# A Mamba layer's normalising and output products by column halves of TensorE, with the planner's TensorE prices by tiling and 62 moved kinds of operations

## The chip, the cores and the metric

The kernel runs on one core of a Trainium2 chip. The metric is the device time of one launch in microseconds. The kernel before takes 8540.97 us, the median of 3 runs (8536.66 to 8543.05). Of a core's engines the text names TensorE (PE; its weight loads are shown apart as PEld), VectorE (DVE), ScalarE (ACT), GpSimd (POOL) and SyncE (SP), whose queue issues most DMAs.

## The reference

The input x is 4 x 128 x 64 x 64 (four images of 128 channels, 4096 tokens each). Two layers follow each other; the first is what the change touches.

```python
# layer 0
x = x + conv_attn_hybrid(group_norm(x), ...)     # seed Mamba, cascade of two Mambas, convolution ffn
# layer 1
t = to_tokens(x)
t = t + attention(ln(t), ...)                    # 4 heads of 32
t = t + moe(ln(t), ...)                          # 8 experts, top 2
```

Layer 0 projects the image onto 8 seed channels and runs a small Mamba over them; it splits the normalised 128 channels into 8 groups of 16 and runs a cascade of two Mambas over each group; it mixes the groups and ends with an ffn that has a 3 x 3 depthwise convolution. One Mamba is:

```python
def _mamba(x, in_w, in_b, conv_w, conv_b, A_log, D, dt_bias, rms_w, out_w, headdim, d_state):
    zxbcdt = x @ in_w.T + in_b
    z, xBC, dt = ...                              # dt through softplus
    xBC = _silu(conv1d(xBC) + conv_b)             # causal, 3 taps
    xs, Bm, Cm = ...
    y = _ssd(xs * dt[..., None], dt * A, Bm, Cm)  # chunks of 64: Yd within, Yo from the carried state
    y = y + D[None, None, :, None] * xs
    y = y.reshape(b, l, di) * _silu(z)
    y = y * jax.lax.rsqrt(jnp.mean(y * y, -1, keepdims=True) + 1e-05) * rms_w
    return y @ out_w.T
```

The mean of y * y and the last product, y @ out_w.T, are the two products that the change reshapes.

## The kernel before

Tokens are worked on in blocks of 512 (LB), each of 8 chunks of 64 (Q). A block of one Mamba is an item. There are 8 seed items (all four images at once) and 64 cascade items: 4 images x 2 Mambas x 8 blocks, where the second Mamba of an image follows the first two blocks behind. The 8 channel groups of a cascade item are 8 lanes, in ng = 2 groups of four; a seed item has 4 lanes and ng = 1.

An item passes four stages, each a Python generator: outer (load x, normalise, split into a high and a low half, store to hl), prep (dt and its running sum acs), front (the input projections ps_z, ps_x, ps_B, ps_C; the masked product gm of B and C; the chunk states ps_st; their scan cd; the part ps_yo from the carried state) and back (the exponentials e from ps_d, their weighing with gm, the product of e and x in the PSUM banks that the profile calls bank and the code py, the gate zs, and at the end `product("ps_ms", ...)` and `product("ps_out", ...)`). At any step the back of one item, the front of the next, the prep of the one after and the outer of the one after that are recorded in turn, and beside them the ffn of the image before (stage ffn).

Nothing is issued while it is recorded. The class Deck collects every call as an Op; neighbouring TensorE calls with one output and one source become one Op (record, L800). `price` gives an Op a duration, from a formula or, for three tiles, from the table SIDE (L763) per matmul, and every TensorE Op has 0.1 us on top. `flush` (L879) then simulates the five engines: each takes, of its Ops whose inputs are there and whose buffers are free, the one first in line, and the order in which the Ops start is the order in which they are issued. The place in line is the recorded number plus an offset from BEHIND (L869), by stage and engine, or by stage, engine and tile: positive is later, negative earlier. One step of the scan records about 150 of them (the trace has some 4100 VectorE, 3000 ScalarE and 500 GpSimd instructions and 2400 groups of matmuls for 66 steps). [...] All recorded operations carry line L996 in the profile, the line that issues them, and are told apart by their tiles.

The two products (lines 699 to 704) add up over the lane groups in one PSUM tile: for each group a full 128 x 128 stationary operand whose columns outside that group's lanes are zero.

Buffers: gm has 3 (4 KB a partition each), xg (the loaded x) 3, acc (the convolution's sum) 2 plus depth, outs 3 plus depth; wide PSUM tiles (tag d: ps_z, ps_x, ps_B, ps_C, ps_ea, pt_b, ps_g, ps_st, ps_yo, ps_d) share 2. The ffn of the last image runs after the scan with depth 1, beside the projections of the attention, and is planned by a second flush.

Of the kernel before, what the change touches and what calls it, by code (L numbers as in the profile page):

```python
# [31 lines left out]
LB = 512  # L32
NBLK = L // LB
Q = 64
# [241 lines left out]
class Mamba:  # L276
# [161 lines left out]
    def front(self, it):  # L438
# [68 lines left out]
        for U in range(NU // 2):  # L507
# [29 lines left out]
            for i in range(2):  # L537
                for jj in range(2):
                    for g in range(ng):
                        for c in range(2):  # L540
                            t = 2 * (2 * U + i) + c
                            for q in range(2):
# [3 lines left out]
                                                 start=True, stop=True)  # L546
            gm = work.tile([128, 4, 2, ng * Q], F32, tag="gm", bufs=3, name="gm")
            nc.vector.tensor_mul(gm.rearrange("s a q x -> s q a x"), d.rearrange("s q u h g l -> s q (u h) (g l)"),
# [72 lines left out]
    def back(self, it, out):  # L621
# [77 lines left out]
        def product(name, lhsT, rhs):  # L699
            p = sh.ps(name)  # L700
            for g in range(ng):
                nc.tensor.matmul(p.rearrange("p (c u l) -> p c u l", c=2, l=Q), lhsT=lhsT[:, g, :], rhs=rhs[:, g],
                                 start=g == 0, stop=g == ng - 1)
            return p
# [45 lines left out]
class Op:  # L750
    __slots__ = ("engine", "calls", "cost", "deps", "users", "waits", "ready", "rank", "uses", "set",
                 "phase", "stage", "out", "src", "both")

    def __init__(self, engine):
        self.engine, self.calls, self.cost, self.deps, self.users = engine, [], 0.0, set(), []
        self.ready, self.rank, self.uses, self.set, self.phase = 0.0, 0.0, {}, None, None
        self.out = self.src = None
        self.both = False
# [3 lines left out]

SIDE = {"py": 0.030, "ps_yo": 0.0185, "ps_d": 0.08}  # L763


class Deck:
# [33 lines left out]
    def record(self, engine, name, args, kw):  # L800
# [8 lines left out]
        if not (op is not None and op.engine == engine and (  # L809
                engine == "tensor" and op.out == made and op.src == src or gelu and op.set == GELU)):  # L810
            op = Op(engine)
            op.out, op.src = made, src
            op.cost = 0.1 if engine == "tensor" else 0.0
            op.stage = self.stage
            op.phase = self.phase if engine in ("tensor", "scalar") else None
            self.ops.append(op)
# [17 lines left out]
    def price(self, engine, name, args, kw, out, ins, op):  # L834
# [4 lines left out]
        if engine == "tensor":  # L839
            tile = op.out.rsplit("_", 1)[0]  # L840
            if tile in SIDE:
                return SIDE[tile]
            lhs = kw.get("lhsT", ins[0])
            single = lhs.dtype == F32R
            side = (128 // max(32, lhs.ap[0][1])) * (128 // max(32, free(lhs)))
            if name == "transpose":
                return 0.12
            return max(0.0165, 0.00046 * n / side) * (1 if single else 2) * (1 if single or side > 1 else 1.85)
# [20 lines left out]
    BEHIND = {  # L869
        ("prep", "tensor"): 150, ("prep", "scalar"): 20,  # L870
        ("front", "vector"): 20,
        ("back", "vector"): -20,
        ("outer", "scalar"): 190, ("outer", "tensor"): -20, ("outer", "vector"): 60, ("outer", "gpsimd"): 60, ("outer", "sync"): 60,
        ("ffn", "vector"): 120, ("ffn", "scalar"): -10, ("ffn", "tensor"): -30, ("ffn", "gpsimd"): -30, ("ffn", "sync"): -30,
    }
    LAG = 0.2
    LAND = 4.0

    def flush(self, tc):  # L879
# [29 lines left out]
        for i, op in enumerate(ops):  # L909
            if op.waits == 0:  # L910
                heappush(events, (0.0, 0, i))
        now, table, lock = 0.0, None, None
        lockers = {"vector": 0.0, "gpsimd": 0.0}
        while events:
# [16 lines left out]
            for e in engines:  # L931
# [3 lines left out]
                while ready[e]:  # L935
# [12 lines left out]
                    if any(room[r] < k for r, k in need.items()) or any(  # L948
# [5 lines left out]
                        aside.append(key)  # L954
                        continue
                    chosen = key
                    break
# [10 lines left out]
                for t in [t for t in op.uses if t not in opening]:  # L968
                    opening.add(t)
                    room[self.ring_of[t]] -= 1  # L970
                    head[self.ring_of[t]] = head.get(self.ring_of[t], 0) + 1
                start = now
                if e == "scalar":
                    if op.set == SILU:
                        phases[op.phase] -= 1
                        lock = op.phase if phases[op.phase] else None
                    if op.set is not None and op.set != table:
                        table = op.set
                        start += 1.3
# [130 lines left out]
def layer0(tc, T, td, const, ident, eps, where, batches, qkv):  # L1110
# [9 lines left out]
    with ExitStack() as ctx:  # L1120
# [63 lines left out]
        def load(b, k, work=work):  # L1184
            xin = work.tile([128, LB], F32, tag="xg", bufs=3, name="xin")
            nc.sync.dma_start(out=xin, in_=T["x"][b, :, blk(k)])
            return xin
# [25 lines left out]
        class Seed:  # L1213
# [3 lines left out]
            def outer(self):  # L1217
# [4 lines left out]
                for b in range(NBATCH):  # L1222
                    normed(b, xs[b])
                    nc.tensor.matmul(pg[32 * b:32 * b + 32, :], lhsT=P("tok"), rhs=xs[b], start=True, stop=True)
                    if b < 2:
                        xs.append(load(b + 2, k))
                g = work.tile([128, LB], F32, tag="xg", bufs=3, name="g")
                nc.vector.tensor_scalar(g, pg, P("tokb"), None, ALU.add)
# [84 lines left out]
        def ffn(b, work, ps, depth=0, diag=0, taps=None, ps_taps=None):  # L1313
# [84 lines left out]
            def conv(k):  # L1398

                accs[k] = []  # L1400
                for g in range(2):
                    acc = work.tile([128, LB], F32, tag="acc", bufs=2 + depth, name="acc")
                    sums = made[k].pop(0) if k in made else None
# [90 lines left out]
        def single(tag, bufs):  # L1494
            return lambda name: pp.tile([128, LB], F32, tag=tag, bufs=bufs, name=name)

        pending = deck.staged("ffn", ffn(pending, last, single("f", 4), 1, 4, taps, single("t", 2)))
        run((pending, FFN), (deck.staged("early", early()), 5 * NBLK + 7))
# [503 lines left out]
```

## Time and profile before

| | us |
|---|---|
| median of 3 runs | 8540.97 |
| profiled execution, with what lies around its span | 8550.11 |
| its span | 8548.1 |
| TensorE busy over the span | 7815.6 (91%) |
| VectorE | 6321.3 (74%) |
| ScalarE | 5117.9 (60%) |
| GpSimd | 4775.4 (56%) |
| scan of the items with no ffn beside it, 348 to 1297: TensorE busy | 815.01 of 949.00 |
| scan with ffn beside it, 1297 to 3440: TensorE busy | 1877.58 of 2143.00 |
| last ffn and first projections, 3440 to 3880: TensorE busy | 380.23 of 440.00 |
| rest, attention and experts, 3880 to 8548: TensorE busy | 4516.45 of 4668.00 |

Shares over the whole span mix two stages: until about 3880 us the first layer, after it the attention, where GpSimd is over 90% busy. What is changed must be read from the first 3880 us. Durations of matmul records overlap, so a step is read from its start to the start of the next. The seed items come every 34 us, the cascade items every 47 to 57 us. The column after a bar is the engine's idle time before such instructions and what ended it.

### The profile page before, as it was taken

What the parts mean: (1) busy time and instruction counts of PE and PEld (TensorE: products, weight loads), DVE (VectorE), ACT (ScalarE), POOL (GpSimd) and SP (SyncE); (2) the same over time, 40 slices, a digit from 0 to 9 for tenths busy, and PEclk for the clock granted to TensorE, in tenths of its full rate; (3) what the DMA queues carried; (4) which work ended last, traced back from release to release, by engine and by line L of the source; (5) the groups of instructions that cost most, each with busy time, mean ns of one, the idle gap of its engine ahead of it and who ended that gap; (6) DMA issues with size and microseconds to landing.
All of it is one profiled execution on the core that took longest, in us unless ns stands there. A gap on an engine that the chain in (4) does not pass through costs nothing.

```text
span 8548.1 us, 191291 instructions
## 1 busy us (share of the span) xinstructions
PE 7815.6 (91%) x80284; PEld 4646.5 (54%) x80284; DVE 6321.3 (74%) x11211; ACT 5117.9 (60%) x6448; POOL 4775.4 (56%) x3225
## 2 busy tenths in 40 slices
PE   5888888888888888888999999999999999999998
PEld 3566666666666666644455555555555555555554
DVE  5666666787777777777777777777777777777775
ACT  5766666777677767764555555555555555555554
POOL 1111110111111111105999999999999999999997
PEclk8989999999989998998999999999999999999999
DMA  4211111111111111125554454545445445444442
GB/s 136 86 48 46 41 40 45 55 51 54 49 52 51 54 49 51 49 90 140 128 128 126 120 126 129 129 126 132 125 124 132 127 124 130 121 114 117 118 122 62
DMA packets 306604, 800.54 MB, mean 94 GB/s; under 512 B 43984, under 2 KB 61008, under 8 KB 288848
## 3 DMA queue, kind: packets, MB, share of 16 engines
q1 hardware_dynamic: 304848, 780.94, 34.7%
q8 instruction: 633, 10.37, 0.5%
q10 hardware_dynamic: 432, 5.12, 0.2%
q14 instruction: 227, 1.86, 0.1%
q0 software_dynamic: 464, 2.25, 0.1%
HBM read 595.19 MB, written 192.94 MB: 92 GB/s over the span
## 4 chain that ended last, share of the span: by engine, by line
PE 30%; POOL 20%; issue 3%; DVE 3%; ACT 1%; DMA 0%; POOLq 0%; DVEq 0%; SPq 0%; ACTq 0%
POOL s L1850 12%; PE ps_mx L1806 7%; PE acc L1865 6%; PE ps_s L1844 6%; POOL es L1852 5%; PE ps_s L1838 3%; PE ps_e L1754 2%; PE ps_den L1878 2%; DVE mx L1808 1%; PE ps_taps L996 1%; POOL parts L1668 0%; PE ps_sh L1825 0%; PE ps_f L1743 0%; POOL cx L1670 0%; PE ps_f L1742 0%
## 5 line engine op out<-in xcount | busy, mean ns | idle before, releaser
L1808 DVE TENSOR_REDUCE mx<-ps_mx 128x1 f32<-128x512 f32 x4096 | 2790.8, 689 | 815.1 <-PE ps_mx L1806 788.7
L1848 ACT ACTIVATE e<-ps_s 128x1024 f32<-128x1024 f32 x2048 | 1986.6, 1022 | 1722.1 <-PE ps_s L1844 1594.0
L1850 POOL TENSOR_TENSOR s<-e 128x1024 f32<-128x1024 f32 x1024 | 2442.6, 2385 | 217.8 <-ACT e L1848 214.0
L1806 PE MATMUL ps_mx<-k,q 128*128 128x512 f32 x4096 | 1881.1, 469 | 60.4 <-DVE mx L1808 28.0
L1852 POOL TENSOR_TENSOR es<-s 128x512 f32<-128x512 f32 x1024 | 1311.7, 1281 | 80.3
L1844 PE MATMUL ps_s<-q,k 128*128 128x512 f32 x4096 | 1282.4, 394 | 0.0
L1865 PE MATMUL acc<-e,V 128*32 128x512 f32 x8192 | 1095.2, 607 | 0.0
L1806 PEld LDWEIGHTS ps_mx<-k,q 128*128 128x128 f32 x4096 | 775.5, 189 | 531.8 <-DVE mx L1808 222.1
L1844 PEld LDWEIGHTS ps_s<-q,k 128*128 128x128 f32 x4096 | 773.5, 189 | 139.2 <-issue 2.9
L996 DVE SCALAR_TENSOR_TENSOR y<-bank,const,y 128x128 f32<-128x128 f32 (+1 forms) x1152 | 355.3, 338 | 589.0 <-PE bank L996 586.4
L996 DVE SCALAR_TENSOR_TENSOR e<-e,gm 128x1024 f32<-128x1024 f32 (+1 forms) x576 | 656.7, 1161 | 69.3 <-ACT e L996 68.5
L1838 PEld LDWEIGHTS ps_s<-mr,ones 32*128 32x128 f32 x4096 | 200.9, 181 | 890.8 <-ACT e L1848 418.7
L996 PE MATMUL bank<-e,xp 64*32 64x128 f32 x17408 | 592.9, 276 | 36.1 <-DVE y L996 27.0
L996 POOL TENSOR_TENSOR zs<-y,zs 128x1024 f32<-128x1024 f32 (+1 forms) x72 | 182.4, 2533 | 780.1 <-DVE y L996 780.0
L996 ACT ACTIVATE e<-ps_d 128x1024 f32<-128x1024 f32 (+1 forms) x576 | 548.1, 976 | 116.1 <-PE ps_d L996 107.1
L1838 PE MATMUL ps_s<-mr,ones 32*128 32x512 f32 x4096 | 532.1, 496 | 20.4 <-ACT e L1848 20.4
L996 PEld LDWEIGHTS bank<-e,xp 64*32 64x32 f32 x17408 | 439.2, 108 | 165.7 <-DVE y L996 58.4
L996 PE MATMUL ps_d<-rt,lt 32*128 32x256 f32 x4352 | 373.0, 307 | 26.8 <-ACT e L996 9.8
L996 POOL CAST x<-halo_casc 128x8 fp32r<-128x8 f32 x64 | 17.0, 266 | 663.8 <-PE ps_C L996 663.7
L996 POOL TENSOR_TENSOR u<-acs 128x512 f32<-128x512 f32 x72 | 75.8, 1053 | 516.0 <-DVE acs L996 465.3
L996 PEld LDWEIGHTS ps_d<-rt,lt 32*128 32x128 f32 x4352 | 271.1, 186 | 168.6 <-issue 56.7
L1865 PEld LDWEIGHTS acc<-e,V 128*32 128x32 f32 x8192 | 161.4, 108 | 364.2 <-issue 358.4
(349 smaller groups left out, 12260.5 us busy)
## 6 DMA issues: line engine op xcount, KB each, us to landing
k<-kd SPq DMA_DIRECT2D x512, 512.0 KB, 5.7
x<-hl SPq DMA_DIRECT2D x256, 256.0 KB, 4.0
V<-vd SPq DMA_DIRECT2D x128, 512.0 KB, 9.7
cd<-raw SPq DMA_DIRECT2D x256, 256.0 KB, 3.3
parts<-cd SPq DMA_DIRECT2D x128, 512.0 KB, 6.2
xin<-in_x SPq DMA_DIRECT2D x128, 256.0 KB, 3.2
q<-qd SPq DMA_DIRECT2D x512, 64.0 KB, 4.9
hl<-hi SPq DMA_DIRECT2D x72, 256.0 KB, 2.5
```

The costliest lines, as they stand in the source:

```text
L996: getattr(getattr(self.nc, op.engine), name)(*[self.real(a) for a in args], **{k: self.real(a) for k, a in kw.items()})
L1754: nc.tensor.matmul(pe, lhsT=xl[:, tok], rhs=ew[:, e:e + 2, :].rearrange("p e c -> p (e c)"), start=True, stop=True)
L1806: nc.tensor.matmul(p, lhsT=q4s[u][:, 128 * qt:128 * qt + 128], rhs=k4s[u][:, blk(kb)], start=True, stop=True)
L1808: nc.vector.tensor_reduce(mxs[u][:, qt, kb:kb + 1], p, AX.X, ALU.max)
L1838: nc.tensor.matmul(pts[j // 2][:, j % 2, :], lhsT=ones2[rows, :], rhs=mrows[u][rows, :], start=True, stop=False)
L1844: nc.tensor.matmul(pts[j // 2][:, j % 2, :], lhsT=k4s[u][:, 128 * kt:128 * kt + 128], rhs=q4s[u], start=False, stop=True)
L1848: nc.scalar.activation(e[:, 2 * j:2 * j + 2], pts[j], AF.Exp)
L1850: nc.gpsimd.tensor_add(s2, e[:, 0:2], e[:, 2:4])
L1852: nc.gpsimd.tensor_add(s, s2[:, 0], s2[:, 1])
L1865: nc.tensor.matmul(accs[u][32 * j:32 * j + 32, :], lhsT=Vs[u][:, 4 * g + j, :], rhs=e[:, j, :], start=g == 0, stop=g == 7)
L1878: nc.tensor.matmul(p[32 * j:32 * j + 32, :], lhsT=ones, rhs=s, start=True, stop=True)
```

## The change

`product` writes each lane group's rows of the output (64 of 128 partitions with ng = 2) by its own matmul with a stationary operand of 128 x 64, each with start and stop, and no longer adds up. In the planner, the calls that write the two py banks are joined even where their source e changes; SIDE's values for py and ps_yo are raised; each TensorE Op has a mode (rows and columns of its stationary operand), and 0.1 us is added where it differs from the one before; a candidate in the same mode could be taken first within NEAR places, which is 0. BEHIND has 62 new entries in place of its 14. gm has 2 buffers, xg 4, acc one more; the last ffn runs with depth 0.

```diff
--- before.py
+++ after.py
@@ -544,7 +544,7 @@
                                 nc.tensor.matmul(d[64 * c:64 * c + 64, q, i, jj, g, :],
                                                  lhsT=Bt[rows, 2 * g + jj, t, :], rhs=Ct[rows, 2 * g + jj, t, :],
                                                  start=True, stop=True)
-            gm = work.tile([128, 4, 2, ng * Q], F32, tag="gm", bufs=3, name="gm")
+            gm = work.tile([128, 4, 2, ng * Q], F32, tag="gm", bufs=2, name="gm")
             nc.vector.tensor_mul(gm.rearrange("s a q x -> s q a x"), d.rearrange("s q u h g l -> s q (u h) (g l)"),
                                  const("tri")[:, None, None, 0:ng * Q].to_broadcast([128, 2, 4, ng * Q]))
             gms.append(gm)
@@ -697,10 +697,12 @@
             return t.rearrange("p (u g c l) -> p g c u l", u=NU, g=ng, c=2)
 
         def product(name, lhsT, rhs):
-            p = sh.ps(name)
+
+            p, n = sh.ps(name), 128 // ng
             for g in range(ng):
-                nc.tensor.matmul(p.rearrange("p (c u l) -> p c u l", c=2, l=Q), lhsT=lhsT[:, g, :], rhs=rhs[:, g],
-                                 start=g == 0, stop=g == ng - 1)
+                rows = slice(n * g, n * g + n)
+                nc.tensor.matmul(p[rows].rearrange("p (c u l) -> p c u l", c=2, l=Q), lhsT=lhsT[:, g, rows],
+                                 rhs=rhs[:, g], start=True, stop=True)
             return p
 
         pm = product("ps_ms", self.ms, by_token(y))
@@ -749,18 +751,18 @@
 
 class Op:
     __slots__ = ("engine", "calls", "cost", "deps", "users", "waits", "ready", "rank", "uses", "set",
-                 "phase", "stage", "out", "src", "both")
+                 "phase", "stage", "mode", "out", "src", "both")
 
     def __init__(self, engine):
         self.engine, self.calls, self.cost, self.deps, self.users = engine, [], 0.0, set(), []
         self.ready, self.rank, self.uses, self.set, self.phase = 0.0, 0.0, {}, None, None
-        self.out = self.src = None
+        self.out = self.src = self.mode = None
         self.both = False
 
 
 SILU, GELU, EXPS = "silu", "gelu", "exps"
 
-SIDE = {"py": 0.030, "ps_yo": 0.0185, "ps_d": 0.08}
+SIDE = {"py": 0.0435, "ps_yo": 0.033, "ps_d": 0.08}
 
 
 class Deck:
@@ -807,7 +809,7 @@
         op = self.ops[-1] if self.ops else None
         gelu = AF.Gelu_apprx_tanh in args
         if not (op is not None and op.engine == engine and (
-                engine == "tensor" and op.out == made and op.src == src or gelu and op.set == GELU)):
+                engine == "tensor" and op.out == made and (op.src == src or made != out.tensor.name) or gelu and op.set == GELU)):
             op = Op(engine)
             op.out, op.src = made, src
             op.cost = 0.1 if engine == "tensor" else 0.0
@@ -838,9 +840,10 @@
             return 0.06
         if engine == "tensor":
             tile = op.out.rsplit("_", 1)[0]
+            lhs = kw.get("lhsT", ins[0])
+            op.mode = max(32, lhs.ap[0][1]), max(32, free(lhs))
             if tile in SIDE:
                 return SIDE[tile]
-            lhs = kw.get("lhsT", ins[0])
             single = lhs.dtype == F32R
             side = (128 // max(32, lhs.ap[0][1])) * (128 // max(32, free(lhs)))
             if name == "transpose":
@@ -867,13 +870,31 @@
 
 
     BEHIND = {
-        ("prep", "tensor"): 150, ("prep", "scalar"): 20,
-        ("front", "vector"): 20,
-        ("back", "vector"): -20,
-        ("outer", "scalar"): 190, ("outer", "tensor"): -20, ("outer", "vector"): 60, ("outer", "gpsimd"): 60, ("outer", "sync"): 60,
-        ("ffn", "vector"): 120, ("ffn", "scalar"): -10, ("ffn", "tensor"): -30, ("ffn", "gpsimd"): -30, ("ffn", "sync"): -30,
+        ("back", "gpsimd", "last0_casc1"): 120, ("back", "scalar"): -50, ("back", "scalar", "A_casc1"): -200,
+        ("back", "scalar", "e"): -40, ("back", "sync", "gfd"): -10, ("back", "sync", "hl"): 120,
+        ("back", "sync", "raw"): -40, ("back", "sync", "td"): 110, ("back", "tensor", "ps_d"): -70,
+        ("back", "tensor", "py"): 120, ("back", "vector", "A_casc1"): -200, ("back", "vector", "bdt_casc1"): 70,
+        ("back", "vector", "biasB_casc1"): 40, ("back", "vector", "wc_casc1"): -120, ("ffn", "scalar"): 10,
+        ("ffn", "tensor", "ps_mean"): 40, ("ffn", "vector", "acc"): 140, ("front", "gpsimd"): 220,
+        ("front", "gpsimd", "last_casc1"): -10, ("front", "scalar"): 20, ("front", "scalar", "Bc"): 50,
+        ("front", "scalar", "Cc"): -200, ("front", "scalar", "cd"): 200, ("front", "scalar", "zs"): -70,
+        ("front", "tensor"): 20, ("front", "tensor", "ps_ea"): -120, ("front", "tensor", "ps_g"): -120,
+        ("front", "tensor", "ps_st"): -20, ("front", "tensor", "pt_x"): 40, ("front", "vector", "gm"): 10,
+        ("front", "vector", "ps_st"): -20, ("front", "vector", "xd"): -200, ("front", "vector", "xp0"): -10,
+        ("outer", "gpsimd"): -200, ("outer", "gpsimd", "halo_seed"): 200, ("outer", "gpsimd", "last0_casc0"): 120,
+        ("outer", "scalar"): 40, ("outer", "scalar", "hi"): -120, ("outer", "scalar", "ln_r"): -20,
+        ("outer", "sync", "raw"): 20, ("outer", "sync", "wc_seed"): 20, ("outer", "sync", "xin"): -40,
+        ("outer", "tensor"): 110, ("outer", "tensor", "ps_tok"): 40, ("outer", "vector"): -20,
+        ("outer", "vector", "A_seed"): 200, ("outer", "vector", "W_casc0"): 200, ("outer", "vector", "bdt_casc0"): 10,
+        ("outer", "vector", "bdt_seed"): 10, ("outer", "vector", "biasB_casc0"): 20,
+        ("outer", "vector", "biasB_seed"): -10, ("outer", "vector", "biasx_seed"): 200,
+        ("outer", "vector", "raw"): 70, ("prep", "gpsimd"): 70, ("prep", "gpsimd", "cdx"): 10,
+        ("prep", "gpsimd", "halo_seed"): 10, ("prep", "gpsimd", "x4"): -40, ("prep", "scalar", "cde"): -70,
+        ("prep", "sync", "x4"): 40, ("prep", "tensor", "ps_cd"): 10, ("prep", "vector", "acs"): -190,
+        ("prep", "vector", "sdT"): -70,
     }
     LAG = 0.2
+    NEAR = 0
     LAND = 4.0
 
     def flush(self, tc):
@@ -909,7 +930,7 @@
         for i, op in enumerate(ops):
             if op.waits == 0:
                 heappush(events, (0.0, 0, i))
-        now, table, lock = 0.0, None, None
+        now, table, lock, mode = 0.0, None, None, None
         lockers = {"vector": 0.0, "gpsimd": 0.0}
         while events:
             now = events[0][0]
@@ -953,6 +974,17 @@
                             e == "gpsimd" and lockers["vector"] > now + 1e-9):
                         aside.append(key)
                         continue
+                    if e == "tensor" and chosen is None and op.mode != mode:
+
+                        chosen = key
+                        continue
+                    if chosen is not None and (op.mode != mode or key[0] - chosen[0] > self.NEAR):
+                        aside.append(key)
+                        if key[0] - chosen[0] > self.NEAR:
+                            break
+                        continue
+                    if chosen is not None:
+                        aside.append(chosen)
                     chosen = key
                     break
                 for key in aside:
@@ -970,6 +1002,9 @@
                     room[self.ring_of[t]] -= 1
                     head[self.ring_of[t]] = head.get(self.ring_of[t], 0) + 1
                 start = now
+                if e == "tensor" and op.mode != mode:
+                    mode = op.mode
+                    start += 0.1
                 if e == "scalar":
                     if op.set == SILU:
                         phases[op.phase] -= 1
@@ -1182,7 +1217,7 @@
         gfd = dram.tile([128, L], F32, name="gfd")
 
         def load(b, k, work=work):
-            xin = work.tile([128, LB], F32, tag="xg", bufs=3, name="xin")
+            xin = work.tile([128, LB], F32, tag="xg", bufs=4, name="xin")
             nc.sync.dma_start(out=xin, in_=T["x"][b, :, blk(k)])
             return xin
 
@@ -1224,7 +1259,7 @@
                     nc.tensor.matmul(pg[32 * b:32 * b + 32, :], lhsT=P("tok"), rhs=xs[b], start=True, stop=True)
                     if b < 2:
                         xs.append(load(b + 2, k))
-                g = work.tile([128, LB], F32, tag="xg", bufs=3, name="g")
+                g = work.tile([128, LB], F32, tag="xg", bufs=4, name="g")
                 nc.vector.tensor_scalar(g, pg, P("tokb"), None, ALU.add)
                 nc.sync.dma_start(out=gfd[:, blk(k)], in_=g)
                 yield
@@ -1399,7 +1434,7 @@
 
                 accs[k] = []
                 for g in range(2):
-                    acc = work.tile([128, LB], F32, tag="acc", bufs=2 + depth, name="acc")
+                    acc = work.tile([128, LB], F32, tag="acc", bufs=3 + depth, name="acc")
                     sums = made[k].pop(0) if k in made else None
                     for i in range(diag, 9):
                         w = P("dw")[:, 9 * g + i:9 * g + i + 1]
@@ -1494,7 +1529,7 @@
         def single(tag, bufs):
             return lambda name: pp.tile([128, LB], F32, tag=tag, bufs=bufs, name=name)
 
-        pending = deck.staged("ffn", ffn(pending, last, single("f", 4), 1, 4, taps, single("t", 2)))
+        pending = deck.staged("ffn", ffn(pending, last, single("f", 4), 0, 4, taps, single("t", 2)))
         run((pending, FFN), (deck.staged("early", early()), 5 * NBLK + 7))
         deck.flush(tc)
 
```

## The prediction

> **What bounds the kernel now.** I read the totals by stretch first, because the change touches only the first layer, which ends near 3880 us.
>
> ```profile
> 100.00:3440.00 3340.00, 2892.01 (x49945) 2047.91 (x49947) 2405.36 (x4111) 2328.70 (x3076) 442.55 (x498) 0.91 0.19 53
> 3440.00:3800.00 360.00, 305.08 (x4355) 194.72 (x4352) 277.32 (x449) 231.72 (x312) 50.07 (x42) 0.93 0.19 57
> 3800.00:8548.00 4748.00, 4591.60 (x25795) 2389.72 (x25793) 3590.70 (x6523) 2524.22 (x3005) 4271.15 (x2652) 0.99 0.48 123
> ```
>
> The columns are length, then busy time of TensorE, its weight loads, VectorE, ScalarE and GpSimd, then TensorE's clock and the DMA share. Between 100 and 3440 us TensorE is busy 87% of the time, VectorE 72% and ScalarE 70%: TensorE is nearest to the bound, but 448 us (3340 - 2892) of it is idle, and its clock is 0.91 on average where the last stage has 0.99. The attention stage after 3880 us has no changed line and I leave it at its time.
>
> The list of TensorE's waits in the same stretch says where the idle time is:
>
> ```profile
> PE ps_st L996 <- DVE gm L996: 97.4, 40, 4.6
> PE ps_var L996 <- ACT ln_r L996: 61.5, 22, 4.8
> PE ps_ms L996 <- ACT y L996: 37.7, 11, 5.1
> PE pt_x L996 <- DVE xp L996: 30.6, 16, 3.4
> ```
>
> The largest stands once in most items of the Mamba scan. The timeline of TensorE in one such item (start, length, count), and then that of VectorE just before the wait ends:
>
> ```profile
> 1029.82 1.16 PE L996 MATMUL ps_g<-Cc,Bc 64*64 64x64 f32 x64
> 1034.96 3.46 PE L996 MATMUL ps_st<-xd,bT 64*64 64x32 f32 x128 [3.98 <-DVE gm L996]
> 1038.36 3.78 PE L996 MATMUL ps_ms<-y,const 128*128 128x512 f32 x4
> 1041.93 0.50 PE L996 MATMUL ps_cd<-cdx,const 128*128 128x160 f32 x2
> 1042.97 1.98 PE L996 MATMUL ps_out<-zs,wc_casc 128*128 128x512 f32 x4 [0.55 <-ACT y L996]
> 1044.79 0.60 PE L996 MATMUL pt_sd<-ident,sd 128*128 128x128 f32 x4
> ```
>
> ```profile
> 1032.58 1.22 DVE L996 TENSOR_TENSOR_SCAN acs<-const,rl 128x512 f32<-128x512 f32 x1
> 1033.71 1.20 DVE L996 TENSOR_TENSOR gm<-ps_g,const 128x1024 f32<-128x1024 f32 x1
> ```
>
> Two things are to be seen. TensorE stands for 3.98 us because VectorE takes the other items' work (up to the scan acs) ahead of gm. And the four records of ps_ms right after it take 3.57 us (1038.36 to 1041.93), those of ps_out, of the same shape, 1.82 us (1042.97 to 1044.79): the idle gap costs clock too. The groups by shape give the same over all items:
>
> ```profile
> L996 PE MATMUL ps_ms<-y,const 128*128 128x512 f32 x248 | 182.6, 875 | 44.1 <-ACT y L996 37.7 <-DVE g L996 4.7 <-DVE outs L996 1.5
> ...
> L996 PE MATMUL ps_out<-zs,wc_casc 128*128 128x512 f32 x232 | 114.6, 617 | 13.6 <-ACT y L996 11.2 <-DVE cds L996 2.4
> ```
>
> **What the Trainium skill says.** "TensorE: Matmul & The Clock Gate", Part 1, says that an idle window of about 3.4 us halves TensorE's clock until it has been busy about as long again; the trace agrees (3.57 against 1.82 us after the 3.98 us gap). "TensorEngine Tiling (Array Packing)", Key Properties, says that tiles run independently and that changing the tiling mode drains TensorE; its Performance Considerations give a stationary operand of 64 columns or fewer a factor of up to two. The trace has no matmul of 128 x 64, but it has the one of 128 x 32:
>
> ```profile
> 72.89 1.06 PE L996 MATMUL ps_tok<-xin,pb 128*32 128x512 f32 x6
> 73.87 1.45 PE L996 MATMUL ps_B<-x,W_seed 128*128 128x512 f32 x5
> ```
>
> Six records, three products in three column groups, take 0.98 us to the next start, where six full ones would take 2.73 (6 x 1.82/4): the groups do run side by side, two records deep.
>
> **The change part by part.** 64 cascade items (4 batches x 2 layers x 8 blocks) matter; the 8 seed items have one group and keep their full-width products.
>
> *Products on column halves.* Each of ps_ms and ps_out goes from four records of 128 x 128 to four of 128 x 64, two side by side. Two records deep is 0.91 us (half of 1.82); with the drain at the switch in and out I take 1.00, as ps_tok shows. Per item 2 x (1.82 - 1.00) = 1.64, for 64 items 105 us at full clock. Bounds: if the halves do not overlap, 1.82 plus a drain of about 0.1 each, a loss of 13 us (128 x 0.1); if ps_ms stays on the slow clock it saves more: 182.6 us for 62 items is 2.95 each, which would become about 1.6, so (1.35 + 0.82) x 64 = 139. I take 105.
>
> *One record for both halves of py.* The scheduler's unit for the products with e becomes 64 matmul records, not 32. In TensorE's timeline a group of 32 takes 1.01 us to the next start (1017.65 to 1018.66), one of 16, in a seed item, 0.57 (186.51 to 187.08): 0.44 for 16 and a fixed 0.13. Four joins per item save at most 4 x 0.13 x 64 = 33; nothing at the lower end, where the two halves were adjacent anyway. I take 25. VectorE needed both halves before it could add to y, so no reader becomes later.
>
> *TensorE's prices in the planner.* This adds no instruction; it moves them. The old prices were 0.58 us for a group of py (16 x 0.030 + 0.1) that takes 1.01, and 1.28 for ps_yo (64 x 0.0185 + 0.1) that takes 2.07 (1045.32 to 1047.39). Eight and one of these per item make the old plan 4.2 us per item too short on TensorE (8 x 0.43 + 0.79), of about 50 us (ps_z to ps_z, 999.53 to 1049.86). The new ones, with 0.1 for a switch, are 1.59 for 64 records against 1.89 (0.13 + 4 x 0.44), and 2.31 against 2.07: off by about 1 us per item (4 x 0.30 - 0.24). But the new product is priced at 0.67 (2 x 0.2355 + 0.2) where I expect 1.00, another 0.7. Window NEAR is 0, so no operation is picked for its tiling unless two stand exactly level.
>
> *The 62 moved kinds.* Ahead of the wait on gm: gm goes from 20 places behind while y was 20 ahead, to 10 behind and 0, so it gains 30 places on y; prep's acs goes 190 ahead, xd 200 ahead. py goes 120 back and e's exponentials 90 ahead, so that TensorE keeps products in stock for the place where it now stands. Prep's tensor operations lose a delay of 150. SP's queue moves too: the stores hl of back go 120 back and td 110 back; their readers are the x loads of the item after next, 50 us away, so I cost that at nothing; if the cover fails, GpSimd's halo copy, at the head of its queue, is late and all of prep with it. GpSimd is 13% busy here; front's 220 back delays inj and last, which hold the scan cd and so ps_yo.
> What can be won is 448 us of idle and the slow clock: a clock of 0.91 means 18% of 3340 at half speed, 601 us, of which TensorE's excess is at most 300. From the groups, ps_ms alone loses 1.13 per item (2.95 - 1.82), 72 us; with ps_st behind the same gap (3.40 us here) I estimate 150 in all. From -100 (new stalls) to +450 can come of it. I take a fifth of the 600 us (448 + 150), 120: the gap at gm is one wait with one cause, and 97.4 us of wait with 72 of clock hang on it.
>
> *Buffers.* gm has 3 and gets 2 (4 KB a partition each); xg and acc get one more each (2 KB). In the timeline both gm follow the last multiplication of e (1027.13 + 1.22 = 1028.35 against 1033.71), so the third is unused by 5.4 us and I cost it at nothing; it limits how far gm can be pulled ahead. The one more xg lets the fourth xin load at the start (55.66 against 49.91 us for the third) come some 5 us earlier, once; acc takes a wait from VectorE that is small (2.2 us on ps_f). In the last ffn outs goes from 4 to 3 with acc unchanged at 3: 440 us of stretch, plus or minus 10, taken as nothing.
>
> Sum: 105 + 25 + 120 = 250 us. Against the profiled execution (8550.1 with what lies around its span of 8548.1) that gives 8300; the median of the runs is 9 lower (8540.97), so 8290.
>
> **Rivals.**
> - *The gaps close.* If py in stock covers the 3.98 us gap, the clock stays up and two thirds of the 600 go: 130 + 400 = 530 at best, I say 450, so 8090. For it: one gap per item holds most of both losses. Against: VectorE has 44 of 52 us busy in the items with ffn, and the chain y, zs on GpSimd (3.2 us), square, ps_ms, two ScalarE steps, ps_out remains.
> - *The freed time turns into waiting.* TensorE gets shorter, and the chain just named and that from acs to pt_sd set the item; only some 60 is left, so 8480. For it: ps_ms and ps_out stand inside these chains, among 448 us of waits. Against: they also get shorter with them.
> - *Slower: two buffers for gm.* With py pushed back, weighing e (the reader of gm) gets later, the next item's gm must wait for it, and ps_g holds one of two wide PSUM tiles; everything that TensorE has queued behind (ps_st, ps_d) stands. At 4 us per item, what the gm gap costs now, that is 256 - 130 = 126 slower, about 8660. It decides from 2 us per item (130/64).
>
> **How the numbers follow.** The forecast has a chance of 0.53 (8170 to 8420), the closed gaps 0.18, the freed time waiting 0.17 (nearly all faster), slower 0.10, and 0.02 no change. Within 0.2% (17 us) is what a measurement here cannot tell from none. Faster: 0.53 + 0.18 + 0.17 = 0.88. The range 8070 to 8490 leaves out half of the closed-gap case (0.08), the slower one (0.10) and little else.
>
> **What would show it.** Each product: 128 x 64, and at most 1.0 us to the next start. The clock between 100 and the layer's end: over 0.93 if gaps close; 0.91 or less speaks for waiting. The wait of ps_st on gm: under 60 us; over 97 is the buffer rival. Items: 50 to 52 us now, 47 to 48.5 forecast. It is wrong if the attention stage (3880 on) changes length by over 20 us, or if products take 1.8.

## The result and the profile after

The changed kernel takes 8416.77 us (median of 4 runs, 8406.15 to 8434.42) against 8542.01 of the kernel before (four runs as well): a ratio of 0.9854, with a 95% interval of 0.9834 to 0.9875. That is 125 us faster where 250 were forecast. The time lies inside the forecast's range; the gain is half of what was worked out.

The profiled execution after is 140 us shorter than the one before (8408.0 against 8548.1). Busy time by stretch, first the kernel before, from its first cascade item to its last ps_out and from there to the first matmul of the attention (columns as in the first view of the prediction):

```profile
347.60:3710.80 3363.20, 2927.53 (x51216) 2090.62 (x51214) 2444.55 (x4050) 2328.51 (x3016) 452.14 (x481) 0.92 0.18 49
3710.80:3920.60 209.80, 160.65 (x434) 73.15 (x433) 153.45 (x229) 121.69 (x193) 16.21 (x19) 0.90 0.44 136
```

The same stretches after, and with them the rest:

```profile
332.50:3555.60 3223.10, 2741.25 (x51216) 1988.59 (x51214) 2465.76 (x4056) 2308.14 (x3010) 413.31 (x481) 0.91 0.19 51
3555.60:3788.80 233.20, 173.33 (x432) 75.56 (x432) 147.41 (x223) 119.70 (x192) 17.30 (x19) 0.86 0.39 124
...
3788.80:8408.00 4619.20, 4498.63 (x25536) 2345.16 (x25536) 3496.18 (x6400) 2454.18 (x2896) 4260.40 (x2640) 0.99 0.48 122
```

The stretches are called the scan, the tail and the attention from here on. The scan is 140 us shorter, the tail 23 longer, the start 15 shorter (332.5 against 347.6; what shortened it was not traced). The attention is 8 shorter (4627.5 before), within what it varies by between the runs below (4610.8 to 4629.0). TensorE is busy 186 us less in the scan, and yet it idles 46 us more (481.9 against 435.7), at a clock that is no higher.

TensorE's longest waits in the scan before:

```profile
PE ps_st L996 <- DVE gm L996: 89.7, 37, 4.6
PE ps_var L996 <- ACT ln_r L996: 62.1, 22, 4.8
PE ps_ms L996 <- ACT y L996: 45.4, 13, 5.1
PE pt_x L996 <- DVE xp L996: 33.0, 17, 3.4
```

and after:

```profile
PE ps_ms L1031 <- ACT y L1031: 222.9, 55, 7.6
PE bank L1031 <- DVE y L1031: 56.2, 85, 2.4
PE ps_yo L1031 <- DVE cd L1031: 36.9, 21, 4.0
```

The wait of ps_st on gm is down to 6.4 us. The prediction listed all four, over a slightly different window, and worked with this one alone; but with it went the waits of ps_var on ln_r (none is left) and of pt_x on xp (2.0). One wait took their place: that of ps_ms on y, 222.9 us where it was 45.4. One item in TensorE's timeline:

```profile
885.10 1.16 PE L1031 MATMUL ps_g<-Cc,Bc 64*64 64x64 f32 x64
886.08 0.95 PE L1031 MATMUL ps_st<-xd,bT 64*64 64x32 f32 x50
887.87 1.36 PE L1031 MATMUL ps_st<-xd,bT 64*64 64x32 f32 x78 [0.85 <-issue]
893.10 1.97 PE L1031 MATMUL ps_ms<-y,const 128*64 128x512 f32 x4 [3.87 <-ACT y L1031]
895.01 0.90 PE L1031 MATMUL ps_cd<-cdx,const 128*128 128x160 f32 x2
895.84 0.65 PE L1031 MATMUL ps_yo<-Cc,last_casc 64*32 64x64 f32 x16
...
899.08 1.08 PE L1031 MATMUL ps_out<-zs,wc_casc 128*64 128x512 f32 x4
900.08 0.74 PE L1031 MATMUL ps_d<-rt,lt 32*128 32x256 f32 x8
```

and the chain that ps_ms waits for, from the timeline of all engines:

```profile
888.96 0.34 DVE L1031 SCALAR_TENSOR_TENSOR y<-bank,const,y 128x128 f32<-128x128 f32 x1
...
889.61 2.35 POOL L1031 TENSOR_TENSOR zs<-y,zs 128x1024 f32<-128x1024 f32 x1
...
891.99 1.06 ACT L1031 ACTIVATE y<-zs 128x1024 f32<-128x1024 f32 x1 [1.58 <-POOL zs L1031]
```

The same chain in the item of before that the prediction shows:

```profile
1032.74 3.20 POOL L996 TENSOR_TENSOR zs<-y,zs 128x1024 f32<-128x1024 f32 x1 [13.12 <-DVE y L996]
...
1035.98 1.06 ACT L996 ACTIVATE y<-zs 128x1024 f32<-128x1024 f32 x1 [1.32 <-POOL zs L996]
```

ps_st no longer waits for gm, runs early, and TensorE then stands 3.87 us before ps_ms, about as long as it stood before ps_st (3.98). Before, the stand at ps_st covered this chain: the last step, the square of y on ScalarE, ended at 1037.04, 1.3 us before ps_ms could start behind ps_st. From the start of the second ps_g of an item to that of ps_ms were 8.5 us (1029.82 to 1038.36) and are 8.0 (885.10 to 893.10). The half clock follows the stand to its new place: ps_ms takes 1.91 us to the next start (893.10 to 895.01), about twice the 1.00 of ps_out, the same shape, a little later (899.08 to 900.08). Of the 64 ps_ms, 4 ran without half clock.

For comparing runs I take TensorE's time in the scan apart into three, worked out from the trace: idle; work at full clock, which is its busy time weighted with the granted clock; and clock loss, the rest of the busy time.

| scan of | length | idle | work at full clock | clock loss | ratio to before (95%) |
|---|---|---|---|---|---|
| before | 3363 | 436 | 2713 | 215 | 1 |
| after | 3223 | 482 | 2505 | 237 | 0.9854 (0.9834 to 0.9875) |
| e1_products | 3489 | 552 | 2605 | 332 | 1.0140 (1.0123 to 1.0157) |
| e5_sameorder | 3335 | 463 | 2610 | 262 | 0.9965 (0.9956 to 0.9974) |
| e6_fullsame | 3317 | 482 | 2611 | 225 | 0.9933 (0.9916 to 0.9949) |
| e7_nojoin | 3266 | 425 | 2603 | 237 | 0.9897 (0.9881 to 0.9914) |
| e2_oldorder | 3328 | 522 | 2488 | 319 | 0.9957 (0.9941 to 0.9974) |
| e13_moves | 3346 | 433 | 2712 | 201 | 0.9950 (0.9934 to 0.9967) |
| e3_tail | 3227 | 481 | 2504 | 241 | 0.9820 (0.9804 to 0.9837) |
| e8_buffers | 3249 | 490 | 2506 | 253 | 0.9847 (0.9831 to 0.9864) |
| e4_gate | 3260 | 470 | 2499 | 291 | 0.9859 (0.9842 to 0.9875) |
| e9_warm | 3193 | 341 | 2707 | 145 | 0.9786 (0.9769 to 0.9802) |
| e12_gatewarm | 3220 | 386 | 2642 | 193 | 0.9813 (0.9797 to 0.9830) |
| e10_warmtail | 3182 | 343 | 2710 | 129 | 0.9767 (0.9751 to 0.9783) |

Lengths and parts are those of one traced execution each, the ratios those of medians. Executions of one kernel lie 6 to 35 us apart, so a small difference between two lengths says little by itself.

After against before: 208 us less work, given back in part by 46 of idle time and 22 of clock.

### The profile page after: what moved, and what is told of

Same layout as the page of the kernel before. It is cut to its first block, busy times and chain, and to the rows that moved or that the text cites. A ratio compares the mean times of both kernels' runs of the same rounds, so it can differ in the third digit from the quotient of the medians.

```text
span 8408.0 us, 191225 instructions
## 1 busy us (share of the span) xinstructions
PE 7635.6 (91%) x80284; PEld 4548.2 (54%) x80284; DVE 6326.8 (75%) x11211; ACT 5095.5 (61%) x6444; POOL 4737.9 (56%) x3225
## 4 chain that ended last, share of the span: by engine, by line
PE 51%; POOL 25%; DVE 10%; ACT 7%; issue 5%; DMA 2%; SPq 0%; POOLq 0%; DVEq 0%; ACTq 0%
POOL s L1885 14%; PE ps_mx L1841 7%; POOL es L1887 6%; PE acc L1900 6%; PE ps_s L1879 5%; PE bank L1031 4%; PE ps_s L1873 3%; PE ps_x L1031 2%; PE ps_B L1031 2%; PE ps_d L1031 2%; DVE y L1031 2%; PE ps_C L1031 2%; PE ps_yo L1031 2%; DVE e L1031 2%; POOL zs L1031 1%
## 5 line engine op out<-in xcount | busy, mean ns | idle before, releaser
L1031 PE MATMUL bank<-e,xp 64*32 64x128 f32 x17408 | 473.3, 283 | 62.6 <-DVE y L1031 59.1
L1031 PE MATMUL ps_d<-rt,lt 32*128 32x256 f32 x4352 | 422.4, 317 | 52.1 <-ACT y L1031 15.1
L1031 PEld LDWEIGHTS bank<-e,xp 64*32 64x32 f32 x17408 | 373.1, 110 | 145.7 <-DVE y L1031 99.3
L1031 PEld LDWEIGHTS ps_d<-rt,lt 32*128 32x128 f32 x4352 | 306.4, 195 | 222.3 <-ACT e L1031 49.9
L1031 PE MATMUL ps_ms<-y,const 128*64 128x512 f32 (+1 forms) x272 | 133.7, 1033 | 237.7 <-ACT y L1031 233.7
```

The costliest lines, as they stand in the source:

```text
L1031: getattr(getattr(self.nc, op.engine), name)(*[self.real(a) for a in args], **{k: self.real(a) for k, a in kw.items()})
```

## The experiments

**The products.** First they went alone into the kernel before (the diff of `product`, nothing else).

> The kernel before with the new product alone; planner, offsets and buffers stay as before. Theory A (freed matmul time reaches the end where TensorE does not stand behind another wait): both products at about 1.0 us to the next start where the clock is up, some 105 us less work at full clock, and the time falls by 60 to 120 us. Theory B (ps_ms and ps_out end waits that others set): under 40 us, with the wait of ps_st on gm (97 us) and of ps_ms on y (38 us) as long or longer.

It became 119 us slower (8674.04 against 8555.48), though its work fell by 108 us, about what theory A wanted. Neither theory had this. The product's code also changes the price that the planner computes for it, and so the whole order. The next run has the new product too, but holds the price:

```diff
+            if tile in ("ps_ms", "ps_out"):
+                return 0.00046 * n * 2 * 1.85
```

> The kernel before with the new product, but the planner is told the old duration for it, so that every engine's queue holds the same operations in the same order as before; only the two products are shorter. Theory A (the products as such save time; run e1_products was slower because the planner, given the new price, made another order that suits the chip worse): faster than before by 30 to 110 us, and the slowness of e1_products is the order's. Theory B (shorter products make TensorE stand and lose its clock): within 20 us of before, or slower, with the clock of the scan below 0.91.

The traces agree that the order held: every engine works through the same sequence of groups as before (12151 on TensorE, 6352 on VectorE), though the products are shorter. Ratio 0.9965, 30 us: the lower edge of theory A. The same matmuls in two orders differ by 1.75% (1.0140 and 0.9965), 150 us, so the slowness was the order's. But even in the old order 103 us less work (2713 to 2610) shortens the scan by only 29; 27 went into idle time and 47 into clock loss. Theory B's mechanism is seen beside A's, and its sign for the clock (0.90 in this scan) was right.

The opposite way round, in the changed kernel; mode and price stay those of the new product:

```diff
-                rows = slice(n * g, n * g + n)
-                nc.tensor.matmul(p[rows].rearrange("p (c u l) -> p c u l", c=2, l=Q), lhsT=lhsT[:, g, rows],
-                                 rhs=rhs[:, g], start=True, stop=True)
+                nc.tensor.matmul(p.rearrange("p (c u l) -> p c u l", c=2, l=Q), lhsT=lhsT[:, g, :], rhs=rhs[:, g],
+                                 start=g == 0, stop=g == ng - 1)
```

> The changed kernel with the old full-width product, each queue in the changed kernel's order. Theory A (TensorE's work sets the time): slower than the changed kernel by 80 to 120 us, the 105 us of work back. Theory B (ps_ms stands behind the chain y, zs, square, so what its product saves is lost in the stand and the clock): slower by under 50 us.

The ratio is 0.9933, which is 0.79% or 67 us slower than the changed kernel's 0.9854. The work rises by 106. The time lies between the two expectations: by the ratios two thirds of the product's work reach the end in the new order (the two traced scans differ by more, 94 us), and in the old one less than a third. The wait of ps_ms on y is as in the changed kernel (223.5 us), so it is not the product that makes it.

**The joined py.**

```diff
-                engine == "tensor" and op.out == made and (op.src == src or made != out.tensor.name) or gelu and op.set == GELU)):
+                engine == "tensor" and op.out == made and op.src == src or gelu and op.set == GELU)):
```

> The changed kernel with the two halves of py as two entries again, which the planner may part. Theory A (one piece of 64 records takes 1.50 us where two of 32 take 2.02, 0.5 us four times in each of 64 items): TensorE's work at full clock rises by 60 to 130 us where the planner parts them, and the time by 40 to 120 us. Theory B (the join saves little, the forecast's 25 us): under 30 us slower.

Theory A for the work, 98 us more (2603 against 2505); the time is 0.43% or 37 us longer, just under its edge, as TensorE idles 57 us less in that order. Where the work went is in TensorE's timeline after, where 64 records take 1.49 us to the next start:

```profile
873.48 1.56 PE L1031 MATMUL bank<-e,xp 64*32 64x128 f32 x64
874.97 1.09 PE L1031 MATMUL pt_b<-ident,Bc 128*128 128x128 f32 x8
```

Two groups of 32 with another tile between them took 2.02 before (2 x 1.01). It is standing next to each other that counts, not being one entry: the kernel before has 393 single groups of 32 in its scan and 58 pairs that happened to be neighbours, and such a pair takes 1.50 us there too (504.77 to 506.26; the median of the 19 pairs with neither a stand nor half clock). About 196 parted pairs at 0.52 us are 102 us, an estimate that fits the 98. Why neighbours are faster was not tried apart.

**The moves.** The 14 old offsets in the changed kernel, and the 62 new ones in the kernel before (each the table BEHIND of the other kernel, whole; its first entries in the second case):

```diff
-        ("prep", "tensor"): 150, ("prep", "scalar"): 20,
-        ("front", "vector"): 20,
...
+        ("back", "gpsimd", "last0_casc1"): 120, ("back", "scalar"): -50, ("back", "scalar", "A_casc1"): -200,
...
```

> The changed kernel with the 14 old offsets in place of the 62. Theory A (the moves removed the stand at ps_st, but the stand at ps_ms took its place, so that the gain is the products and the joined py): at most 40 us slower than the changed kernel, the wait of ps_st on gm back at 80 to 130 us and that of ps_ms on y below 100 us. Theory B (the moves carry the gain): slower by 80 us or more.

> The kernel before with the 62 new offsets alone: old product, old prices, old buffers. Theory A (the offsets suit the plan of the new prices only): no faster than before, or slower by up to 150 us. Theory B (they pull gm and acs ahead whatever the prices are): the wait of ps_st on gm under 40 us and the time 30 to 100 us under before.

e2_oldorder is 1.03% or 88 us slower than the changed kernel, so the moves carry that much (its theory B); the wait of ps_st on gm is back at 91.8 us and that of ps_ms at 59.4, as theory A said. e13_moves is 42 us faster than before (theory B, in the time and in the wait), and the shift of the stand is plainest in it. Its waits of TensorE in the scan:

```profile
PE ps_ms L1013 <- ACT y L1013: 253.1, 61, 6.5
PE ps_f L1013 <- ACT acc L1013: 28.5, 6, 10.6
PE bank L1013 <- DVE y L1013: 23.7, 58, 1.0
```

The wait on gm fell from 89.7 to 5.5 us with the moves alone, and the idle time of the scan stayed (436 and 433). Its traced scan is only 17 us shorter than before's; as many lie in the attention, which has no changed line (4610.8 against 4627.5).

**The buffers.** The changed kernel cuts the depth of the last ffn, so that outs has 3 there and not 4. e3_tail gives that stretch alone its old counts, with `load` taking 3 there; e8_buffers gives all tiles theirs.

```diff
-                    acc = work.tile([128, LB], F32, tag="acc", bufs=3 + depth, name="acc")
+                    acc = work.tile([128, LB], F32, tag="acc", bufs=3, name="acc")
...
-        pending = deck.staged("ffn", ffn(pending, last, single("f", 4), 0, 4, taps, single("t", 2)))
+        pending = deck.staged("ffn", ffn(pending, last, single("f", 4), 1, 4, taps, single("t", 2)))
```

> The changed kernel with the last ffn's buffers as before (outs 4, acc 3, xg 3; depth 1); the scan's buffers stay changed. Theory: the 23 us by which the stretch from the last ps_out to the first ps_mx grew (209.8 to 233.2 us) come from outs having 3 and not 4, so the stretch falls back to 205 to 215 us and the time by about 20 us. Rival: they come from the new offsets of stage ffn, and nothing changes.

> The changed kernel with all buffers as before (gm 3, xg 3, acc 2, last ffn with outs 4). Theory A (the scan does not need the third gm nor the extra xg and acc): the tail falls by about 20 us and the scan stays within 15 us of the changed kernel's 3223. Theory B (two gm hold the scan): the scan falls by over 15 us. Theory C (xg or acc pay): the scan grows by over 15 us.

e3_tail is 0.34% (29 us) under the changed kernel by the ratios, whose intervals just touch; the tail itself falls from 233 to 217 us, just over the expected range. The loads of outs, in the tail of before (from 3710.8), after (3555.6) and e3_tail (3557.2), with first and last start:

```profile
L996 SPq DMA_DIRECT2D outs<-td x8: 319/376/649, 3714.8 to 3834.7; - x8
```
```profile
L1031 SPq DMA_DIRECT2D outs<-td x8: 319/320/443, 3567.2 to 3725.8; - x8
```
```profile
L1031 SPq DMA_DIRECT2D outs<-td x8: 319/326/570, 3568.8 to 3688.3; - x8
```

The last load starts 124, 170 and 131 us into the tail, later with three outs. The rival, the new offsets of stage ffn, has nothing for it: e13_moves has them with four outs, and its tail is 206 us. Over all runs the tail is 224 to 236 us with three outs and 206 to 226 with four. In e8_buffers the tail is 219 us and the traced scan 26 longer than the changed kernel's, which is theory C, but weakly: against e3_tail, with a tail as short, it is 0.27% or 23 us slower with intervals that touch, and the planner makes another order for it. Whether xg, acc or that order costs them is not shown. That two gm hold the scan (theory B) finds no support.

**The chain and the clock.** e4_gate multiplies the gate in quarters:

```diff
+        def gate(u):
+            part = slice(2 * ng * Q * u, 2 * ng * Q * (u + 1))
+            nc.gpsimd.tensor_mul(zs[:, part], y[:, part], zs[:, part])
...
             within(u)
+            gate(u)
...
-        nc.gpsimd.tensor_mul(zs, y, zs)
```

> The changed kernel with the gate zs multiplied in four quarters, each as soon as its quarter of y is complete, in place of one multiplication of 2.4 us after the last. Theory A (the chain last py, y, zs, square, ps_ms sets where TensorE stands): the wait of ps_ms on y falls from 211 us to about 100 (1.8 us less for each of 64 items), and the time by 50 to 120 us. Theory B (another wait of the item ends right behind it): the wait of ps_ms falls, another one grows by as much, time within 25 us.

Theory B: the wait of ps_ms fell to 156 us, those of ps_yo on cd and of ps_ea on e rose (60.4 and 38.2, from 36.9 and 22.4), the clock loss rose by 54, and the time is the changed kernel's (0.9859). The planner makes another order of the four smaller operations on all engines, so the run does not show what a shorter chain does in the same order.

e9_warm puts spare matmuls ahead of ps_ms, in the same planner entry and at a price of nothing, so that the order stays (VectorE, ScalarE and GpSimd work through the changed kernel's sequence); they run while TensorE stands:

```diff
+            for _ in range(12 if name == "ps_ms" and ng == 2 else 0):
+                nc.tensor.matmul(p, lhsT=self.W[:, 0:128], rhs=self.W[:, 0:LB], start=True, stop=True)
```

> The changed kernel with twelve spare matmuls (weights by weights, about 0.24 us each) into the tile of ps_ms ahead of its product, in the same queue order: they compute nothing that is used and only keep TensorE at work while it stands for y. Theory A (the half clock that follows the stand costs time): the clock of the scan rises from 0.91 to 0.95 or more, ps_ms, ps_cd and ps_yo run at full speed, and the time falls by 50 to 140 us. Theory B (the chain of the other engines sets the item and the slow matmuls lie beside it): the clock rises, the time stays within 25 us.

Theory A: 0.9786, 0.68% or 58 us faster than the changed kernel by the ratios, with 202 us of useless work more (the two traced scans differ by 30 us; the traced execution is the slowest of four). The clock of the scan is 0.95. An item in its TensorE timeline:

```profile
884.28 3.02 PE L1035 MATMUL ps_ms<-W_casc 128*128 128x512 f32 x12
888.61 1.08 PE L1035 MATMUL ps_ms<-y,const 128*64 128x512 f32 x4 [1.32 <-ACT y L1035]
889.62 0.54 PE L1035 MATMUL ps_cd<-cdx,const 128*128 128x160 f32 x2
890.09 0.43 PE L1035 MATMUL ps_yo<-Cc,last_casc 64*32 64x64 f32 x16
```

ps_ms takes 1.01 us here and ps_cd 0.47, against 1.91 and 0.83 in the changed kernel's item, and 57 of the 64 ps_ms run without half clock. The chain is no shorter: from the second ps_g to ps_ms are 8.06 us (8.00 in the changed kernel), and the stand of 1.32 us is what the spare matmuls leave of it. The gain lies behind it: from ps_ms to ps_out are 4.23 us (888.61 to 892.84) in place of 5.98 (893.10 to 899.08). Over the scan the clock loss falls by 92 us, while idle time and spare work together come to 543 us where 482 were idle.

The last two put these edits together: e12_gatewarm the gate in quarters, the old tail and the spare matmuls, with range(8) in place of range(12); e10_warmtail the old tail and all twelve:

> The same with eight spare matmuls and the gate in four quarters. Theory A (with the clock kept up, a shorter chain y, zs, square does pay): faster than e10_warmtail by 15 us or more. Theory B (the stand moves to ps_yo, which waits for the scan cd on VectorE): within 15 us of e10_warmtail or slower, the wait of ps_yo on cd above 50 us.

Theory B: 0.9813 against 0.9767, with the wait of ps_yo on cd at 55.4 us. The shorter chain does not pay here either. Whether that is the chain, the other order that the planner makes of it or the four fewer spare matmuls of each item (its clock loss is 193 us against 129) is not told apart.

> The spare matmuls of e9_warm and the last ffn's buffers of e3_tail together. Theory: the two lie in different stretches and add up: about 50 us from the clock and 16 to 20 from the tail under the changed kernel, so 180 to 205 us under before. Rival: the tail's gain or the clock's is a matter of one order, and the sum is less than 150.

8354.9 us against 8549.08, 194 us: as the theory said. This is the fastest version by its median, 0.9767 of before, and beats both kernels; from e9_warm (0.9786) its interval does not part it.

## Why the prediction was right in direction and wrong in size

- **What bounds the kernel.** Right that TensorE is nearest to the bound, and that it stands at gm with a slow clock behind it. Wrong in treating the stand as "one wait with one cause": e13_moves took the wait away, and the scan's idle time stayed at 433 us.
- **Idle time and clock, 120 us.** This is the step that failed. The forecast took "a fifth of the 600 us" of idle time and slow clock as gain; the scan lost 68 us more to them (46 + 22). The wait on gm went, as forecast (under 60 us; it is 6.4), and the chain y, zs, square took its place at ps_ms, which waits 223 us where it waited 45. That was the second rival, "the freed time turns into waiting", named with this very chain but priced at some 60 us of gain in all; with 208 us of work less and 68 lost again the scan gained 140.
- **Adding the terms.** The sum took saved work as time, and a gain from the waits on top. The moves can be worth what was forecast: against e2_oldorder, which has the old offsets and all else of the change, the changed kernel has 122 us less idle time and clock loss. But in that run 225 us less work than before had brought 190 us more of both. Added to the kernel before, the moves lower them by 17 us (e13_moves).
- **Products, 105 us.** As work the size was right: 1.01 us each without half clock, and 103 and 106 us in e5_sameorder and e6_fullsame. As time they gave 30 us in the old order and 67 in the new.
- **Joined py, 25 us.** Mis-sized as work, 98 us in all. The forecast took a fixed 0.13 us per group as what a join saves; a parted pair costs 0.52 more than neighbours. As time it is 37 us in e7_nojoin.
- **Luck.** Two misses offset each other in part: the sum has 73 us of py's work too little and 188 us too much for idle time and clock (120 to gain, 68 lost). Without the join, by e7_nojoin, some 88 us of gain would be left and not 125.
- **Prices in the planner.** They were counted as moving operations and given no cost of their own. e1_products shows what a price alone can do: 150 us between two orders of the same matmuls.
- **Buffers at nothing.** Nothing speaks against it for gm. Wrong for the last ffn: the tail grew by 23 us, of which e3_tail has 16 back.
- **Slower by two gm buffers.** Did not come; there is no sign of it in e8_buffers.
- **The signs named.** The clock (0.91) and the items (50 us on average, 3223 for 64; before it was 53) both said "waiting", as the prediction had set out.
- **A reading.** VectorE's "44 of 52 us" in the items with ffn holds for the fuller ones. Over that stretch its mean is 39 of 52 (1616.97 us busy of 2143, from 1297 on), so that argument against closed gaps was weaker than it looked.

The Trainium skill, "TensorE: Matmul & The Clock Gate", Part 1, says that an idle window of about 3.4 us halves the clock. The trace agrees (1.91 us for ps_ms after a stand of 3.87, against 1.01), and e9_warm shows what it costs here. How much of the 140 us each part gave cannot be split without remainder, since each part's gain depends on the order: 67, 37 and 88 us of time by leaving one out, more than the 125 together.

## What to carry to other kernels

When a wait of an engine whose queue has a fixed order is removed, look for what it covered: the next operation in its queue may be waiting for a chain that was hidden until then, and the time to read is from the last free work to the end of that chain, not the wait itself. Work saved on the busiest engine need not become time (here 30 us of 103 in one order, 67 of 106 in another); take idle time, work and clock loss apart before and after, and do not add a gain from waits to one from work as if each were alone. And in a kernel whose order a planner makes, test a shorter operation once with the order held fixed, or the order's effect is read as the operation's.

## What the runs showed that was not expected

- Two groups of 32 records for py take 1.50 us as neighbours and 2.02 with another tile between them, in the kernel before as well.
- Useless matmuls can pay: 64 times twelve of them (202 us of work, most of it in time in which TensorE stood) made the kernel 58 us faster, as the clock loss fell from 237 to 145 us.
- A stand can move without shrinking: with the new offsets alone the wait on gm fell by 84 us, that on y rose to 253, and the scan's idle time changed by 3.
- The same set of matmuls in two planned orders differed by 150 us.
